# Gate logits of a mixture of experts as eight extra columns of the local attention's products

## The chip, the cores and the metric

The kernel runs on one core of a Trainium2 chip. The metric is device time in microseconds (us), as the median of several runs. One further execution was recorded by the hardware profiler; all durations of single instructions come from that one.

## The reference

A small early-fusion model, 16 sequences of 569 rows of 256 numbers, all f32. 441 rows come from image patches (a convolution and one attention head), 128 from text. Layer 0 is what matters here:

```python
h = concatenate([tokenizer(x), txt], axis=1)
h = h + local_attention(layernorm(h))        # windows of 64, shifted by 32, 8 heads
z = layernorm(h)                             # (h - mean) / sqrt(var + 1e-5), no weights
logits = z @ gate_w + gate_b                 # gate_w is 256 x 8
probs = softmax(logits)                      # 8 experts; the two largest are used
h = h + sum_e weight_e * (gelu(z @ W1_e + b1_e) @ W2_e + b2_e)
```

Layer 1 is a linear attention over phases followed by an LSTM over the 569 steps; neither is touched.

Because the layer norm subtracts the mean of a row, the logits can be written without the normalized rows: with `G` the gate weights less the mean of each column, `logits = rstd * (h @ G) + gate_b`. And h after the attention is `h0 + A @ w_out + biases`, so `h @ G = h0 @ G + A @ (w_out @ G) + biases @ G`. The windows already hold the normalized h0, turned, as an operand of TensorE: `h0 @ G = std0 * (layernorm(h0) @ G)`.

## The kernel before

The program has two parts. The first part (to about 950 us) makes the tokens, the window attention and the routing of the rows to experts. The second part runs the experts (79 tiles of 256 rows), then layer 1 and the LSTM.

**Order.** Every engine has a fixed order of instructions, which the program itself works out while it is built. `Order` is a planner: each piece of work is a generator ("stream") that yields an engine and an assumed duration before it issues instructions, for example `yield "PE", 0.44, "64"` (the last word names the tiling mode of TensorE's array, whose changes the planner charges for). The planner always takes next the step that can start first by its own clock. A changed step therefore also changes the order of others. `yield "at", event` waits for a mark that another stream sets; this is order only, the waits on the chip follow from the data.

**Units.** Two sequences make a pair `p` (8 pairs); a pair has 9 chunks of 128 rows, so there are 72 chunks. `H[p, c]` is a chunk's rows, 128 x 256, in 18 rotating buffers.

**Streams of the first part.**

- `setup` is not a stream: it is issued ahead, in program order. It loads the weights, multiplies constant weights together, and makes the bias rows `tok_b` and `win_b` (lines 484 to 490). The tiles of its pool give their room to those of the streams when setup's last use of them is over.
- `features` makes the image features `fT` for each sequence, on ScalarE (ACT, line 505) and VectorE (DVE, line 512); `projections` and two `tokens` streams turn them into rows of `H`.
- `norms` runs the first layer norm of each chunk (`norm`, lines 625 to 638): statistics on DVE, `rstd` on GpSimd (POOL, lines 635 and 636), the normalized rows `wxn` on DVE (line 638). It may be four chunks ahead of the windows.
- Four `windows` streams take the chunks in turn. Each turns `wxn` on TensorE (PE) into `xT`, makes keys and queries (`wqk`), scores (`wsc`), values (`wv`), a softmax over `wS` (DVE, POOL, ACT, DVE), turns it (`wpt`), multiplies by the values (`wav`), and by `wout` (`wob`, line 777); line 779 adds that to `h` in place. All of one stream's products share one PSUM bank, in turn. `h` is stored to `HD` in DRAM by a DMA of SyncE's queue (SP).
- A fork after each chunk, `sent_rows`, runs the second layer norm into `XN`.
- `routing` (lines 785 on) waits for a part's chunks and computes their logits: for two chunks at a time it turns `XN` on PE (`rtr`, line 800) and copies it on ACT (`rxT`, line 804); for up to four chunks it multiplies with the gate weights `gw` in the 32-column mode (`lg`, line 810), copies on ACT (`lgs`, line 816), turns back on PE (`lt`, line 819) and adds the bias on DVE (`pr`, line 821). Then come the softmax over 8 experts and the ranks on DVE, two products that count rows (`pos`), and the scatter of the rows to the experts' regions by POOL's indirect DMAs (`send`, line 908). A part is a pair; the last pair is cut into three parts of 4, 3 and 2 chunks, which makes 10 parts.

When the last part is routed, DVE works out which expert each tile belongs to, SP reads that into registers and fetches weights (line 1168) and rows (line 1174).

Of the kernel before, what the change touches and what calls it, by code (L numbers as in the profile page):

```python
# [17 lines left out]
D = 256  # L18
# [17 lines left out]
    ("bk1", 2), ("bq1", 2), ("bk2", 1), ("bq2", 1), ("ln_w", 2), ("ln_b", 2),  # L36
# [258 lines left out]
def kernel(ctx: ExitStack, tc: tile.TileContext, a: dict, out: bass.AP):  # L295
# [63 lines left out]
    gw = route.tile([128, 2, 32], F32, name="gw")  # L359
# [16 lines left out]
    H, XN, made = {}, {}, []  # L376
# [12 lines left out]
    def rows_of(p, c):  # L389

        while len(made) >= ROWS:
            before = ("normed", *made[len(made) - ROWS])
            if before in first.events:
                break
            yield "at", before
        made.append((p, c))
        H[p, c] = hp.tile([128, D], F32, name=f"h{p}_{c}", tag="h", bufs=ROWS)
        return H[p, c]

    def texts():  # L400

        for p in range(NP):
            if p:
                yield "at", ("token", p - 1, 3)
            for c in (7, 6, 8):
                h = yield from rows_of(p, c)
                if c == 8:
                    yield "POOL", 0.3
                    nc.gpsimd.memset(h, 0.0)
                lo, hi, at = {6: (25, 64, 0), 7: (0, 64, 39), 8: (0, 25, 103)}[c]  # L410
                for s in range(2):
                    nc.sync.dma_start(
                        h[64 * s + lo : 64 * s + hi], a["txt"][2 * p + s][at : at + hi - lo, :]
# [3 lines left out]
    def setup():  # L417
# [12 lines left out]
        nc.scalar.dma_start(wout, a["w_out"].rearrange("(k p) n -> p k n", p=128))  # L430
# [8 lines left out]
        nc.gpsimd.memset(gw, 0.0)  # L439
        nc.scalar.dma_start(gw[:, :, :E], a["gate_w"].rearrange("(k p) n -> p k n", p=128))  # L440
# [42 lines left out]
        for i, (name, w, b, to) in enumerate((("bv", wo, "bo", tok_b), ("vb", wout, "b_out", win_b))):  # L483
            v = tmp.tile([128, 2, 128], F32, name=f"{name}_every")
            for k in range(2):
                nc.vector.tensor_copy(v[:, k, :], col(name, k).to_broadcast([128, 128]))
            mm = place_of(f"{name}_row", 2 + i)
            for k in range(2):
                nc.tensor.matmul(mm[:, :D], v[:, k, :], w[:, k, :], start=(k == 0), stop=(k == 1))
            nc.vector.tensor_tensor(to, mm[:, :D], row(b), ALU.add)  # L490
# [77 lines left out]
    def tokens(slot):  # L568

        last = NIMG - 384  # L570
        for n in range(slot, 7 * NP, 2):
# [46 lines left out]
            for q, i in to:  # L618
                yield "DVE", 0.48
                nc.vector.scalar_tensor_tensor(  # L620
                    H[p, i][q], mm[q], share_[q], tok_b[q], ALU.mult, ALU.add
# [3 lines left out]
    def norm(h, to, name, slot):  # L625
# [3 lines left out]
        nc.vector.bn_stats(st, h)  # L629
# [4 lines left out]
        yield "POOL", 0.85  # L634
        nc.gpsimd.tensor_scalar(rstd, mv[:, 1:2], EPS, None, ALU.add)
        nc.gpsimd.tensor_tensor(rstd, rstd, mhalf[:, :1], ALU.pow)
        yield "DVE+", 0.5
        nc.vector.tensor_scalar(to, h, mv[:, 0:1], rstd, ALU.subtract, ALU.mult)
# [12 lines left out]
    def sent_rows(p, c, h, slot):  # L651

        if p not in XN:
            if p > 1:
                yield "at", ("sent", p - 2)
            if p not in XN:
                XN[p] = xnp.tile([128, NC, WIDE], F32, name=f"XN{p}", tag="XN", bufs=2)
                yield "POOL", 0.2
                nc.gpsimd.tensor_copy(XN[p][:, :, D], cols[:, COL["row"] + NC * p : COL["row"] + NC * (p + 1)])
        yield from norm(h, XN[p][:, c, :D], f"r{p}_{c}", slot)  # L660
# [11 lines left out]
    def windows(slot):  # L672

        kb, vb = KB[slot], VB[slot]
        for n in range(slot, NC * NP, WINDOWS):
# [28 lines left out]
            nc.gpsimd.tensor_tensor(h, h, win_b, ALU.add)  # L704
# [16 lines left out]
            v = place_of(f"wv{u}", slot)[:, :D].rearrange("p (w n) -> p w n", w=2)  # L721
            for w in range(2):
                for k in range(2):
                    yield "PE", 0.22, "64"
                    for odd in range(2):
# [4 lines left out]
                        )  # L730
            top = wk.tile([128, NH], F32, name=f"wtop{u}", tag=f"wtop{slot}", bufs=1)
            yield "DVE", 0.68
            nc.vector.tensor_reduce(top, S, AX.X, ALU.max)
            for odd in range(2):
# [39 lines left out]
            ob = place_of(f"wob{u}", slot)[:, :D]  # L774
            for m in range(2):
                yield "PE", D * COLUMN
                nc.tensor.matmul(ob, AT[:, m, :], wout[:, m, :], start=(m == 0), stop=(m == 1))
            yield "DVE", 0.42
            nc.vector.tensor_tensor(h, ob, h, ALU.add)
            nc.sync.dma_start(HD[p][:, c, :], h)  # L780
# [4 lines left out]
    def routing():  # L785

        for p, lo, hi in PARTS:
            u, n = f"{p}_{lo}", hi - lo
            pr = wk.tile([128, n, E], F32, name=f"pr{u}", tag="pr", bufs=1)
            for g0 in range(lo, hi, 4):  # L790
                m = min(4, hi - g0)
                xT = wk.tile([128, 2, 4, 128], F32, name=f"rxT{p}_{g0}", tag="rxT", bufs=1)
                for c0 in range(g0, g0 + m, 2):
                    two = min(2, hi - c0)
# [1281 lines left out]
```

## Time and profile before

| | |
|---|---|
| median of 3 runs | 3378.91 us (3378.6 to 3380.3) |
| profiled execution | 3360.87 us, its span 3359.0 us |
| granted TensorE clock in it | 0.978 |
| PE busy | 3055.1 us, 91% of the span, 57536 instructions |
| DVE busy | 2027.2 us, 60% |
| ACT busy | 1471.9 us, 44% |
| POOL busy | 786.6 us, 23% |
| moved by DMA | 366.81 MB, mean 109 GB/s |

The span runs from the first to the last instruction of the profiled execution. In a group of instructions the busy time is the union of their spans; spans of neighbours on PE overlap, since matmuls are pipelined. "Idle before" is the time in which the engine stood still just ahead of an instruction, and the name after the arrow is what ended it.

### The profile page before, as it was taken

The page shows a single profiled execution, that of the slowest core. Times are in us where ns is not written, and L with a number is a line of the kernel's source. Part 1 is how long each engine was busy: PE and PEld are TensorE (multiplying, and loading weights), DVE is VectorE, ACT ScalarE, POOL GpSimd, SP SyncE. Part 2 cuts the span into 40 slices and gives each one's busy share as a digit, 9 for nine tenths or more (in the row PEclk, how much of TensorE's full clock was granted, in tenths as well). Part 3 has the DMA queues.
Part 4 walks back from the last instruction along what each step waited for, and adds up shares of the span by engine and source line. Part 5 has one row for each costly group of instructions (what it writes and reads, how often), then busy time and mean ns, then how long its engine had stood idle before and what let it go on. Part 6 is the DMA issues. An engine that isn't in the chain of part 4 may idle for free.

```text
span 3359.0 us, 134328 instructions
## 1 busy us (share of the span) xinstructions
PE 3055.1 (91%) x57536; PEld 2231.5 (66%) x57536; DVE 2027.2 (60%) x6787; ACT 1471.9 (44%) x5030; POOL 786.6 (23%) x1524
## 2 busy tenths in 40 slices
PE   5999999999859999997899999999999999999884
PEld 3666666666548888886566676766666666666652
DVE  4677777766732222222566777777777777766555
ACT  3545545454412222221444555555555555554442
POOL 1243554445533322232311001010101010100000
PEclk9999999999979999998999999999999999999997
DMA  5111221111176666664333333333333333333333
GB/s 180 53 46 57 89 79 54 55 38 41 42 251 234 220 231 225 225 229 141 100 100 88 90 82 86 84 94 78 97 77 92 84 93 79 76 91 80 90 103 113
DMA packets 276070, 366.81 MB, mean 109 GB/s; under 512 B 144480, under 2 KB 220176, under 8 KB 263312
## 3 DMA queue, kind: packets, MB, share of 16 engines
q1 hardware_dynamic: 249360, 300.91, 30.5%
q0 software_dynamic: 14496, 39.75, 3.1%
q10 hardware_dynamic: 11616, 17.56, 1.8%
q8 instruction: 451, 7.39, 0.9%
q14 instruction: 147, 1.20, 0.1%
HBM read 239.33 MB, written 118.75 MB: 107 GB/s over the span
## 4 chain that ended last, share of the span: by engine, by line
PE 37%; DVE 7%; ACT 5%; issue 2%; SPq 1%; DMA 1%; POOL 0%; ACTq 0%; DVEq 0%; POOLq 0%
PE gates L1741 13%; PE xm_False L1085 5%; PE out_gate L1750 2%; PE ek L1085 2%; PE po_False L1085 2%; PE z L1085 2%; PE v L1085 2%; PE eq L1085 2%; PE ds_False L1085 2%; ACT act L1762 1%; PE r_False L1085 1%; ACT th L1798 1%; DVE ab L1777 1%; DVE cT L1790 1%; DVE act L1783 1%
## 5 line engine op out<-in xcount | busy, mean ns | idle before, releaser
L1741 PE MATMUL gates<-W_hh,X 128*16 128x96 f32 (+1 forms) x18176 | 487.9, 248 | 63.9 <-DVE X L1805 61.6
L1741 PEld LDWEIGHTS gates<-W_hh,X 128*16 128x16 f32 (+1 forms) x18176 | 373.6, 103 | 258.5 <-DVE X L1805 245.0
L1248 ACT ACTIVATE hT<-hp,w 128x256 f32<-128x256 f32 x316 | 132.6, 472 | 481.5 <-PE hp L1241 314.5
L1762 ACT ACTIVATE act<-gates 128x96 f32<-128x96 f32 x568 | 142.1, 250 | 444.1 <-PE gates L1741 437.0
L1255 PE MATMUL y<-w,hT 128*128 128x256 f32 x1264 | 289.7, 382 | 5.2 <-ACT hT L1248 1.5
L1085 PE MATMUL xm_False<-W_ih,dxT_False 128*32 128x256 f32 x4352 | 292.3, 380 | 2.3 <-DVE dxT_False L1271 1.9
L1241 PE MATMUL hp<-xt,w 128*128 128x256 f32 x1264 | 287.6, 381 | 1.0 <-ACT hT L1248 1.0
L1777 DVE SCALAR_TENSOR_TENSOR ab<-act 128x64 f32<-128x64 f32 x568 | 127.9, 225 | 258.2 <-ACT act L1762 250.8
L1255 PEld LDWEIGHTS y<-w,hT 128*128 128x128 f32 x1264 | 236.8, 190 | 45.2 <-ACT hT L1248 14.4
L1684 PEld LDWEIGHTS <-nil 128*32 128x32 bf16 x4552 | 190.3, 94 | 111.0 <-issue 53.0
L1241 PEld LDWEIGHTS hp<-xt,w 128*128 128x128 f32 x1264 | 239.9, 191 | 35.7 <-ACT hT L1248 1.5
L1184 POOL DMA_INDIRECT YT<-ys,to x158 | 153.4, 971 | 440.4 <-DVE ys L1261 408.9
L1261 DVE TENSOR_TENSOR ys<-y,w 128x512 f32<-128x512 f32 x79 | 54.6, 691 | 316.3 <-PE y L1255 241.1
L1750 PE MATMUL out_gate<-W_hh,X 128*32 128x64 f32 x9088 | 233.8, 219 | 0.7 <-issue 0.7
L1690 ACT COPY gates<-xc 128x96 f32<-128x96 f32 x569 | 138.6, 244 | 182.0 <-DMA xc<-XCD 75.4
L1750 PEld LDWEIGHTS out_gate<-W_hh,X 128*32 128x32 f32 x9088 | 187.9, 110 | 2.9 <-issue 1.1
L1805 DVE SCALAR_TENSOR_TENSOR X<-toT,th 128x32 f32<-128x32 f32 x569 | 109.9, 193 | 120.5 <-ACT th L1798 116.9
L1798 ACT ACTIVATE th<-cT 128x32 f32<-128x32 f32 x569 | 130.5, 229 | 92.9 <-DVE cT L1790 43.1
L1301 POOL TENSOR_SCALAR d_False_rstd<-d_False_mv 128x2 f32<-128x2 f32 (+1 forms) x36 | 9.0, 250 | 671.8 <-DVE d_False_mv L1293 547.4
L908 POOL DMA_INDIRECT XS<-XN,at x144 | 149.1, 1035 | 45.6 <-issue 24.6
L693 PE MATMUL wqk<-wxT,wqkv 128*128 128x128 f32 x1152 | 150.6, 278 | 8.9 <-ACT wxT L687 8.6
L693 PEld LDWEIGHTS wqk<-wxT,wqkv 128*128 128x128 f32 x1152 | 139.4, 192 | 24.9 <-ACT wxT L687 13.5
(356 smaller groups left out, 6497.9 us busy)
## 6 DMA issues: line engine op xcount, KB each, us to landing
w<-in_wpack SPq DMA_DIRECT2D x79, 1154.0 KB
taps<-in_taps SPq DMA_DIRECT2D x16, 1764.0 KB
xc<-XCD SPq DMA_DIRECT2D x71, 384.0 KB
XCD<-xp_False SPq DMA_DIRECT2D x256, 96.0 KB
xs<-XS SPq DMA_DIRECT2D x79, 258.0 KB
yg<-YT SPq DMA_DIRECT2D x72, 256.0 KB
HD<-h SPq DMA_DIRECT2D x72, 128.0 KB
fh<-HD SPq DMA_DIRECT2D x72, 128.0 KB
```

The costliest lines, as they stand in the source:

```text
L693: nc.tensor.matmul(qk[:, j, m, :], wqkv[:, k, D * j + 128 * m : D * j + 128 * m + 128], xT[:, k, :], start=(k == 0), stop=(k == 1),)
L908: fill(0, nc.gpsimd.indirect_dma_start(out=XS[0], out_offset=bass.IndirectOffsetOnAxis(ap=at[:, i, c - lo : c - lo + 1], axis=0), in_=XN[p ...
L1085: nc.tensor.matmul(out[own], lhsT[:, own], rhs, start=start, stop=stop)
L1184: keep(nc.gpsimd.indirect_dma_start(out=YT, out_offset=bass.IndirectOffsetOnAxis(ap=to[:, i : i + 1], axis=0), in_=ys[:, i, :], in_offset= ...
L1241: nc.tensor.matmul(hp[:, i, :], w1[:, k, hc * 128 : (hc + 1) * 128], xT[:, k, :], start=(k == 0), stop=(k == 1),)
L1255: nc.tensor.matmul(y[:, i, :], hT[:, hc, 128 * i : 128 * i + 128], w2[:, hc, :], start=(hc == 0), stop=(hc == 3),)
L1684: nc.tensor.matmul(g[32 * q : 32 * q + 32, :n], nil[:, :32], nil[:, :n], start=True, stop=last)
L1741: nc.tensor.matmul(GC[32 * q : 32 * q + NB * (1 + half), :96], before[:, kk, NB * (1 - half) :], Whh[:, kk, own : own + 96], start=False, ...
L1750: nc.tensor.matmul(GO[32 * q : 32 * q + 32, :64], before[:, kk, :], Whh[:, kk, own : own + 64], start=False, stop=(kk == 1),)
L1762: nc.scalar.activation(act[:, :96], GC[:, :96], AF.Tanh, scale=0.5), begun.pop((k, t))
L1777: nc.vector.scalar_tensor_tensor(ab, act[:, :64].rearrange("p (g x) -> p g x", g=2), 1.0, act[:, 64:].rearrange("p (g x) -> p g x", g=2), ...
L1798: nc.scalar.activation(th.rearrange("p k x -> p (k x)"), cT, AF.Tanh, scale=0.5)
```

## The change

The gate weights are centred once, in setup, by a product with a matrix of ones and two VectorE operations. `wout` gets eight more columns, `w_out @ G`, by two turns, two copies and two products for each of its halves; `win_b` gets eight more elements, the biases times `G`.

`H` gets nine more columns: eight for the growing logits and one for the standard deviation of the row before the attention. The first layer norm computes that one on POOL, by a third instruction after `rstd`. A window multiplies its `xT` with the centred gate weights just after the values, into eight more columns of the same PSUM bank, and VectorE scales them by the standard deviation and adds the bias. The product with `wout` and the add after it are 264 columns wide instead of 256. After the second layer norm a VectorE operation multiplies by `rstd` and adds `gate_b`, into a new tile `LG`. `routing` reads `LG` and has no step on PE or ACT ahead of its softmax.

```diff
-    gw = route.tile([128, 2, 32], F32, name="gw")
+    gw = route.tile([128, 2, E], F32, name="gw")
...
-        H[p, c] = hp.tile([128, D], F32, name=f"h{p}_{c}", tag="h", bufs=ROWS)
+        H[p, c] = hp.tile([128, D + E + 1], F32, name=f"h{p}_{c}", tag="h", bufs=ROWS)
...
# setup
-        nc.gpsimd.memset(gw, 0.0)
-        nc.scalar.dma_start(gw[:, :, :E], a["gate_w"].rearrange("(k p) n -> p k n", p=128))
+        nc.scalar.dma_start(gw, a["gate_w"].rearrange("(k p) n -> p k n", p=128))
...
+        nc.vector.memset(half, 0.5)
+        mm = place_of("gate_sum", 4)
+        for k in range(2):
+            nc.tensor.matmul(mm[:, :E], ones, gw[:, k, :], start=(k == 0), stop=(k == 1))
+        for k in range(2):
+            nc.vector.scalar_tensor_tensor(
+                gw[:, k, :], mm[:, :E], -1.0 / D, gw[:, k, :], ALU.mult, ALU.add
+            )
+        for m in range(2):
+            mm = place_of(f"wout_t{m}", 5)
+            woutT = tmp.tile([128, 2, 128], F32, name=f"woutT{m}")
+            for k in range(2):
+                nc.tensor.transpose(
+                    mm[:, 128 * k : 128 * k + 128], wout[:, m, 128 * k : 128 * k + 128], ident
+                )
+            nc.scalar.copy(woutT.rearrange("p k n -> p (k n)"), mm[:, :D])
+            mm = place_of(f"wout_gate{m}", 4)
+            for k in range(2):
+                nc.tensor.matmul(mm[:, :E], woutT[:, k, :], gw[:, k, :], start=(k == 0), stop=(k == 1))
+            nc.scalar.copy(wout[:, m, D:], mm[:, :E])
+        every = {}
+        for name in ("bv", "vb", "ob"):
...
+        mm = place_of("bv_row", 2)
+        for k in range(2):
+            nc.tensor.matmul(mm[:, :D], every["bv"][:, k, :], wo[:, k, :], start=(k == 0), stop=(k == 1))
+        nc.vector.tensor_tensor(tok_b, mm[:, :D], row("bo"), ALU.add)
+        mm = place_of("vb_row", 3)
+        for k in range(2):
+            nc.tensor.matmul(mm[:, : D + E], every["vb"][:, k, :], wout[:, k, :], start=(k == 0), stop=False)
+        for k in range(2):
+            nc.tensor.matmul(
+                mm[:, D : D + E], every["ob"][:, k, :], gw[:, k, :], start=False, stop=(k == 1)
+            )
+        nc.vector.tensor_tensor(win_b[:, :D], mm[:, :D], row("b_out"), ALU.add)
+        nc.vector.tensor_copy(win_b[:, D:], mm[:, D : D + E])
...
# norm
-        yield "POOL", 0.85
-        nc.gpsimd.tensor_scalar(rstd, mv[:, 1:2], EPS, None, ALU.add)
-        nc.gpsimd.tensor_tensor(rstd, rstd, mhalf[:, :1], ALU.pow)
+        yield "POOL", 0.85 if name[0] == "r" else 1.28
+        over = mv[:, 1:2]
+        nc.gpsimd.tensor_scalar(over, over, EPS, None, ALU.add)
+        nc.gpsimd.tensor_tensor(rstd, over, mhalf[:, :1], ALU.pow)
+        if name[0] == "w":
+            nc.gpsimd.tensor_tensor(h[:, D + E :], over, half, ALU.pow)
...
# sent_rows
-        yield from norm(h, XN[p][:, c, :D], f"r{p}_{c}", slot)
+        rstd = yield from norm(h, XN[p][:, c, :D], f"r{p}_{c}", slot)
+        yield "DVE", 0.19
+        nc.vector.scalar_tensor_tensor(
+            LG[p][:, c, :], h[:, D : D + E], rstd, frow("gate_b", E), ALU.mult, ALU.add
+        )
...
# windows, after the products of v
+            for k in range(2):
+                yield "PE", 0.06, "64"
+                for w in range(2):
+                    own = slice(64 * w, 64 * w + 64)
+                    nc.tensor.matmul(
+                        vg[own, D : D + E], xT[:, k, own], gw[:, k, :], start=(k == 0), stop=(k == 1)
+                    )
             top = wk.tile([128, NH], F32, name=f"wtop{u}", tag=f"wtop{slot}", bufs=1)
             yield "DVE", 0.68
             nc.vector.tensor_reduce(top, S, AX.X, ALU.max)
+            yield "DVE", 0.2
+            nc.vector.scalar_tensor_tensor(
+                h[:, D : D + E], vg[:, D : D + E], h[:, D + E :], win_b[:, D:], ALU.mult, ALU.add
+            )
...
-            ob = place_of(f"wob{u}", slot)[:, :D]
+            ob = place_of(f"wob{u}", slot)[:, : D + E]
             for m in range(2):
-                yield "PE", D * COLUMN
+                yield "PE", (D + E) * COLUMN
                 nc.tensor.matmul(ob, AT[:, m, :], wout[:, m, :], start=(m == 0), stop=(m == 1))
             yield "DVE", 0.42
-            nc.vector.tensor_tensor(h, ob, h, ALU.add)
-            nc.sync.dma_start(HD[p][:, c, :], h)
+            nc.vector.tensor_tensor(h[:, : D + E], ob, h[:, : D + E], ALU.add)
+            nc.sync.dma_start(HD[p][:, c, :], h[:, :D])
...
# routing
-            pr = wk.tile([128, n, E], F32, name=f"pr{u}", tag="pr", bufs=1)
-            for g0 in range(lo, hi, 4):
-                m = min(4, hi - g0)
-                xT = wk.tile([128, 2, 4, 128], F32, name=f"rxT{p}_{g0}", tag="rxT", bufs=1)
-                for c0 in range(g0, g0 + m, 2):
...
-                            nc.tensor.transpose(
-                                tr[:, k, c - c0, :], XN[p][:, c, 128 * k : 128 * k + 128], ident
-                            )
...
-                    nc.scalar.copy(xT[:, :, c0 - g0 : c0 - g0 + two, :], tr[:, :, :two, :])
...
-                        nc.tensor.matmul(
-                            lg[32 * j : 32 * j + 32, :128], gw[:, k, :], xT[:, k, j, :],
-                            start=(k == 0), stop=(k == 1),
-                        )
...
-                nc.scalar.copy(lgs[: 32 * m], lg[: 32 * m, :128])
...
-                nc.tensor.transpose(lt, lgs[: 32 * m], ident[: 32 * m, : 32 * m])
...
-                nc.vector.tensor_tensor(
-                    pr[:, g0 - lo : g0 - lo + m, :],
-                    lt.rearrange("p (j e) -> p j e", e=32)[:, :, :E],
-                    frow("gate_b", E).unsqueeze(1).to_broadcast([128, m, E]), ALU.add,
-                )
+            for c in range(lo, hi):
+                yield "at", ("normed", p, c)
+            pr = LG[p][:, lo:hi, :]
```

## The prediction

> **What bounds the kernel now.** I read first the 40 slices of the span, to find where the change lives. A digit is the busy share in tenths; a slice is 84 us.
>
> ```profile
> PE   5999999999859999997899999999999999999884
> DVE  4677777766732222222566777777777777766555
> POOL 1243554445533322232311001010101010100000
> ```
>
> The changed work lies in slices 0 to 11, the first stage: tokens, windows, routing. There TensorE (PE) is at nine tenths, VectorE (DVE) at seven and GpSimd (POOL) at four or five. Second, the busy time of the stage's steady part as one stretch:
>
> ```profile
> core 0: us, PE busy (x) PEld busy (x) DVE busy (x) ACT busy (x) POOL busy (x), PEclk, DMA share, GB/s
> 60.00:900.00 840.00, 781.04 (x6887) 547.65 (x6888) 595.54 (x1556) 421.40 (x1144) 376.23 (x658) 1.00 0.17 58
> ```
>
> PE is busy 781 of 840 us and DMA 17%, so PE bounds this stretch, with 59 us of gaps. DVE follows at 71%, ACT at 50%, POOL at 45%. Third, PE's waits there (us in total, times, longest):
>
> ```profile
> PE wpt L754 <- DVE wS L750: 10.0, 9, 2.5
> PE wv L726 <- DVE wS L717: 9.4, 10, 1.9
> PE wqk L693 <- ACT wxT L687: 7.4, 13, 1.4
> PE wtr L683 <- DVE wxn L638: 6.2, 8, 1.6
> ```
>
> The gaps are the windows' own chains, mostly DVE's part of them. The routing's turned rows and gate products are not among the large waits: what they cost is PE time. Fourth, the groups by shape (60 to 950 us): busy time, mean ns of one, idle time before.
>
> ```profile
> L800 PE MATMUL rtr<-ident,XN 128*128 128x128 f32 x144 | 26.3, 287 | 1.3 <-DVE part L887 0.6 <-DVE XN L638 0.5
> L810 PE MATMUL lg<-rxT,gw 128*32 128x128 f32 x288 | 15.7, 283 | 0.9 <-ACT rxT L804 0.7
> L819 PE MATMUL lt<-ident,lgs 128*128 128x128 f32 x15 | 4.8, 323 | 1.5 <-ACT lgs L816 1.5
> L766 PE MATMUL wav<-wPT,VB 128*64 128x64 f32 x1152 | 48.2, 227 | 3.4 <-ACT wPT L759 3.4
> L777 PE MATMUL wob<-wout,wAT 128*128 128x256 f32 x288 | 75.2, 387 | 1.1 <-ACT wAT L773 0.9
> L636 POOL TENSOR_TENSOR w_rstd<-w_rstd,mhalf 128x1 f32<-128x1 f32 x71 | 44.2, 622 | 5.9
> ```
>
> The counts show that one f32 product is two instructions (288 for 144 products) and a turn is one. Neighbours overlap, so group sums are too large; I take the step from start to start in the order of time where I can. Last, the two ends of the stage in order of time (start, us), setup first:
>
> ```profile
> 28.66 0.26 DVE L462 TENSOR_TENSOR mixed<-mixed,ew 128x96 f32<-128x96 f32 x1
> 29.11 2.08 PE L489 MATMUL bv_row<-tok_wo,bv_every 128*128 128x256 f32 x4 [4.55 <-DVE bv_every L486]
> 31.88 2.04 PE L489 MATMUL vb_row<-wout,vb_every 128*128 128x256 f32 x4 [0.70 <-issue]
> 33.97 1.96 ACT L505 ACTIVATE fT<-taps,cols 128x220 f32<-128x220 f32 x4 [9.00 <-PE vb_row L489]
> ```
> ```profile
> 936.36 0.57 POOL L636 TENSOR_TENSOR r_rstd<-r_rstd,mhalf 128x1 f32<-128x1 f32 x1
> 940.11 1.08 PE L800 MATMUL rtr<-ident,XN 128*128 128x128 f32 x4 [0.56 <-DVE part L887]
> 943.41 0.36 PE L819 MATMUL lt<-ident,lgs 64*128 64x64 f32 x1 [0.41 <-ACT lgs L816]
> 963.40 0.91 SPq L1168 DMA_DIRECT2D w<-in_wpack  x2
> ```
>
> At the front the first features wait for setup's last product (9.00 us of ACT's time), so setup is serial. At the back, the last part's logits pass turn, copy, product, copy, turn before DVE can rank them, and the experts' weights are fetched 20 us after that. Setup and tail are latency; the middle is PE throughput.
>
> **What the Trainium skill says.** TensorE: Matmul & The Clock Gate, "LDWEIGHTS (loading the stationary operand)": the load takes about its columns over 1.2 ns, 53 ns for 64 columns. The trace pays less when two 64-column tiles alternate: 64 of wav took 2.01 us from start to start, 31 ns each. TensorEngine Tiling (Array Packing), "Key Properties": a change of tiling mode drains the engine. That agrees in direction: the 32-column gate group costs 0.58 us for 16 instructions (412.65 to the next start at 413.23) and 0.55 us for four (423.37 to 423.92), so most of it is not the products. SBUF — State Buffer, "SBUF: two separate sides": VectorE and GpSimd share a port pair that one of them holds for a whole instruction. The trace shows no such wait by name, so I use it only as a reason for a bound.
>
> **The change part by part.** PE, removed: 144 turns; four took 0.49 us (407.66 to 408.15), so 0.12 x 144 = 17.6 us. 24 gate groups x 0.57 = 13.6. 24 turns back x 0.16 (413.76 to 413.91 and alike) = 3.8. Sum 35 us; the group sums (26.3 + 15.7 + 7.2 = 49) are the upper bound.
>
> PE, added: per chunk two k by two windows, twice for f32, so 8 instructions of 128x64 weights and 8 moving columns, 576 in all. No row has this shape; wav is nearest (same weights, alternating halves, 64 columns) at 31 to 39 ns (2.01/64, 0.63/16). Fewer columns can't beat the load, so I take 35: 20.2 us. Ends: 26 ns, the out_gate products (233.8 us over 9088, 32 columns), 14.8 us; 53 ns, the page's price without overlap, 30.7 us. They follow v's products in the same mode, so I add no switch. The out product grows from 256 to 264 columns: 14 of wob took 3.12 us, 0.87 ns a column, x 8 x 288 = 2.0 us. Net on PE: 35 - 22.2 = **13 us less** (2 to 32).
>
> ACT loses 40 copies of rxT and 24 of lgs, about 28 us; I count nothing, since it is half idle; a shorter ACT queue can only help the 23 us of PE's waits on it. DVE gains two small products per chunk: 144 x 0.19 (the 128x8 reciprocal's 194 ns) = 27 us, less 24 adds (4 us): +23 us, 71 to 74%. POOL gains a third power per chunk in the windows' norms, 72 x 0.57 = +41 us, 45 to 50%. Both lie beside PE's work. Their cover is the four window and two token streams; without it they lengthen the DVE waits above. The new power is queued behind rstd, so DVE's wxn need not wait for it, but POOL's next instruction does (h plus win_b, the softmax subtraction). The new DVE product waits for the gate products; behind it in DVE's order stand the other windows' copies and sums. Against that, DVE no longer stands still for the turned-back logits (7.8 us before 900). I take 0, with -6 to +15.
>
> DMA: the gate weights' load stays at its place on ACT's queue, but setup needs it now instead of at 149 us. Its landing is not shown; the core's traffic is near nothing after 27 us, so it should be there before 28.9. SP's stores of h carry the same 256 columns. The memset of gw on POOL goes, 0.15 us, at a time when POOL is early.
>
> Setup: after "mixed" DVE centres the gates (two, about 0.4 us); then PE product, ACT copy, PE turn, ACT copy, PE product, ACT copy: about 0.5 + 0.3 + 0.5 + 0.5 + 0.6 + 0.3 = 2.7 us on rows of the same setup (four qb products 0.50 us, copies 0.17 to 0.38). The bv row thus starts near 31.9 instead of 29.1, both rows follow back to back (4.2 us instead of 4.8), and four short products with gw close it (0.5 us). The end moves from 33.9 to some 36.7: **+3 us**, ends 0 (PE's clock already up) and +6 (late gate weights). Nothing covers it.
>
> Tail: from the last part's XN (937.4) to its logits (943.8) stand 6.4 us. Now one DVE product of 0.19 us remains, but DVE still has the previous part to finish (941.3), so some 2.5 us come off there. The part before waited 2.7 us for its turned-back logits, and its scatter on POOL held back the last chunk's rstd (DVE waited 2.7 us for it). What is late next is that scatter, 1.27 us a piece. I take **-4 us**, ends -7 and +2.
>
> Sum: -13 + 0 + 3 - 4 = **-14 us**. The profiled execution took 3360.87 us (span 3359.0 plus 1.9), so 3346.9 there. The median of the runs, 3378.91, is 18 us above it, which no part of the change touches; carried over, 3364.9. A measurement of this kernel can tell about 0.2%, 6.8 us, from no change.
>
> **The rivals.** (1) The sum holds, -7 to -22: 50%. (2) The drains are worth the group sums and the routing leaves the streams' way: 49 - 17 on PE, 3 and -4 at the ends, about -30, 3349: 14%. For it: the 32-column group's flat 0.55 us. (3) Cover: PE's removed pieces filled gaps of the window chains, whose length does not change. Then some 5 of the 13 us arrive, -6 in all, 3373, within what can be told: 20%. For it: 59 us of gaps, nearly all in those chains. Against: PE is at 93%. (4) Slower: DVE and POOL take over. Place: wxn and the softmax subtraction behind the third power, on queues where DVE already waits 19.2 us for w_rstd. Price: 41 + 23 = 64 us of new work; from 21 us of it showing up as PE gaps (a third) the kernel is slower by over 0.2%, at half (32) by 18 us, 3397: 16%. Against: the norms run up to four chunks ahead. That the change doesn't do what it says is no case: the routing's PE steps are gone from the code.
>
> **How the numbers follow.** The likeliest is 3365. The range 3350 to 3385 leaves out about half of (2) and most of (4). Faster 0.64 is (1) and (2), same 0.20 is (3), slower 0.16 is (4).
>
> **What would show it.** Right: rtr, lg, lt gone; 576 small products at 30 to 40 ns from start to start; the first fT near 37 us; PE busy some 13 to 25 us less before the experts; weights fetched about 14 us earlier than 963.4. Wrong: small products above 53 ns, more PE waits on wS and wxn, POOL as their releaser, or a later stage moving by more than the first one's shift.

## The result, and the profile after

The change makes the kernel faster by 0.44%: 3363.13 us (median of 6 runs, 3361.35 to 3367.92) against 3378.76 us for the kernel before beside it (6 runs, 3374.59 to 3382.14), ratio 0.9956, 95% interval 0.9943 to 0.9968. That is 15.6 us less, where the forecast was 14 less and 3365. The profiled execution took 3363.40 us, its span 3361.6.

One caution before the lines are read. Another session of runs can give the same kernel some 12 us more or less: before had medians of 3368.94, 3380.29 and 3367.60 in the three sessions of experiments (the first two on one chip, the third on another), while the ratio of the two kernels was 0.9956 here and 0.9958 and 0.9954 in the two sessions in which the change was run again. So total times are compared below only within one session, and the start times in the profile of before quoted in the prediction (3360.87 us) are not set against those of this one of after: their experts start at 972.8 and 971.9 us, which hides nearly the whole gain. A pair from one session follows the views of after.

The page of after, the 40 slices (a digit is the busy share in tenths, a slice is 84 us):

```profile
PE   6999998999759999997899999999999999999884
DVE  4777777786732222222566777777777777776555
POOL 1354465545533322222311001010101010100000
```

POOL rises by one tenth in six of the slices 1 to 8 and falls by one in slice 4, DVE hardly changes, PE not visibly. The shape is that of before. After's steady part as one stretch:

```profile
core 0: us, PE busy (x) PEld busy (x) DVE busy (x) ACT busy (x) POOL busy (x), PEclk, DMA share, GB/s
60.00:900.00 840.00, 777.30 (x7058) 547.92 (x7056) 619.97 (x1676) 397.50 (x1085) 427.25 (x751) 0.99 0.17 60
```

PE is still the bound at 93%. DVE is up 24 us and POOL 51, ACT down 24 against the same stretch of before. After's waits of PE in this stretch (us in total, times, longest):

```profile
PE wav L816 <- ACT wPT L809: 10.6, 16, 1.4
PE wqk L731 <- ACT wxT L725: 7.2, 12, 1.2
PE wpt L804 <- DVE wS L800: 6.3, 10, 1.2
PE wv L765 <- DVE wS L755: 6.0, 14, 0.8
```

The waits on DVE's `wS` became smaller (10.0 and 9.4 us before). At the head stands a wait on ACT's copy of the turned softmax, 2.8 us before. No releaser is POOL. After's groups by shape (60 to 950 us; busy, mean ns of one, idle time before and what ended it):

```profile
L787 ACT COPY VB<-wv 64x256 f32<-64x256 f32 x144 | 52.2, 366 | 135.3 <-DVE h L781 119.3 <-DVE ahead L882 7.2 <-DVE wtop L779 4.1
L668 POOL TENSOR_TENSOR h<-w_mv,half 128x1 f32<-128x1 f32 x71 | 41.8, 589 | 0.0
L774 PE MATMUL wv<-gw,wxT 128*64 128x8 f32 x576 | 26.1, 196 | 0.0
L696 DVE SCALAR_TENSOR_TENSOR LG<-h,r_rstd,flow 128x8 f32<-128x8 f32 x72 | 18.4, 256 | 0.3
L781 DVE SCALAR_TENSOR_TENSOR h<-wv,h,win_b 128x8 f32<-128x8 f32 x72 | 15.5, 218 | 14.4 <-PE wv L774 5.5 <-PE tav L636 3.4 <-remote 1.9
```

`rtr`, `lg` and `lt` are gone, and the 576 small products are there with no idle time ahead of them. Their 26.1 us are spans that overlap those of their neighbours. Their price is seen in after's order of time (start, duration in us):

```profile
416.17 1.09 PE L765 MATMUL wv<-wqkv,wxT 128*64 128x128 f32 x16
417.09 0.35 PE L774 MATMUL wv<-gw,wxT 128*64 128x8 f32 x8
417.38 2.67 PE L636 MATMUL tav<-tV,tPT 57*64 57x256 f32 x20
...
435.22 1.09 PE L765 MATMUL wv<-wqkv,wxT 128*64 128x128 f32 x16 [0.51 <-DVE wS L755]
436.14 0.35 PE L774 MATMUL wv<-gw,wxT 128*64 128x8 f32 x8
436.35 1.06 PE L749 MATMUL wsc<-KB,wq 128*64 128x256 f32 x8
```

From start to start, eight products take 0.21 us when the next work has weights of the same 128x64 shape (436.14 to 436.35) and 0.29 us when the shape changes (417.09 to 417.38). Over the chunks where PE did not stand still behind them the median is 0.20 to 0.21, three quarters are at 0.28 or less. That is 26 ns a product and 15 to 17 us in all.

After's setup in order of time:

```profile
34.48 0.86 PE L515 MATMUL vb_row<-gw,ob_every 128*128 128x8 f32 x4
...
35.43 1.96 ACT L534 ACTIVATE fT<-taps,cols 128x220 f32<-128x220 f32 x4 [4.21 <-PE vb_row L515]
```

The end of the chain is as foreseen: the short products close it, and the first features stand behind them, at 35.4 us.

Now the pair of one session: before run again as `b_third` (median 3367.40) and the change as `a_third` (3354.57). Three stretches: first features to the last attention product of the token part (`tav`); to the last store of `h`; to the experts' first turn of rows. First before, then the change, columns as above (PEclk is the granted TensorE clock, 1.00 the full one):

```profile
33.90:873.80 839.90, 780.36 (x6751) 543.78 (x6753) 587.63 (x1533) 422.95 (x1148) 362.20 (x632) 0.99 0.18 61
873.80:935.00 61.20, 42.65 (x430) 32.16 (x426) 47.20 (x138) 23.65 (x59) 41.81 (x75) 0.94 0.17 60
935.00:974.00 39.00, 4.58 (x22) 3.37 (x22) 15.34 (x77) 4.07 (x13) 16.28 (x30) 0.51 0.82 278
```
```profile
34.90:866.20 831.30, 769.88 (x6960) 540.38 (x6960) 620.42 (x1676) 401.69 (x1096) 411.34 (x724) 1.00 0.18 63
866.20:925.70 59.50, 41.19 (x360) 31.25 (x356) 41.91 (x135) 19.55 (x50) 38.19 (x67) 0.85 0.15 54
925.70:956.50 30.80, 1.03 (x4) 0.95 (x5) 11.95 (x56) 3.23 (x11) 8.56 (x16) 0.50 0.85 270
```

The lengths give the account: setup +1.0, the middle 839.9 to 831.3, -8.6, the last windows -1.7, the tail 39.0 to 30.8, **-8.2**. The experts start 17.5 us earlier.

The split between the first two stretches can't be used as it stands, because the clock differs. The trace records TensorE's clock as granted in full or at half. In the middle, before had half of it in two stretches (33.9 to 48.6 and 461.6 to 468.4 us), the change in one; PE's busy time in them, first before, then the change:

```profile
sum 21.50, PE 14.06 PEld 7.97 DVE 17.20 ACT 8.41 POOL 7.18; mean PE 7.03 PEld 3.98 DVE 8.60 ACT 4.21 POOL 3.59
37.50:44.30 6.80, 3.73 (x6) 1.63 (x6) 5.61 (x16) 2.54 (x6) 2.18 (x4) 0.50 0.46 145
```

PE's work at full clock can be estimated by counting its busy time at half clock as half. The middle then has 773.3 us of PE work before and 768.0 in the change: 5.3 us less, where the busy times say 10.5. The estimate can be tested: the three profiles of before have 778.0, 780.2 and 780.4 us of PE in their middles, and 773.4 to 773.6 at full clock. In the last windows the clock tips the other way, 0.94 before and 0.85 in the change: half clock for 6.8 us in each of the three profiles of before, for 17.8 to 26.8 us in those of the change. Taken together the two stretches had half clock for nearly the same time, 28.3 us before and 24.6 in the change, and can be compared: they are 10.3 us shorter, **901.1 to 890.8**. At full clock PE's work there falls by 11.8 us, 813.8 to 802.0, and its gaps grow by 1.6, 78.1 to 79.7.

How much the gaps grow is the less certain part. The other two profiles of the change have the same PE work at full clock (802.0 and 802.2 us), but gaps of 84.9 and 82.9 us. They come from sessions in which the change took 9 to 13 us more and before 3379 and 3380 us; no profile of before has a total near that.

The stages behind are the same program. In this pair they took 9.3 us longer after the change (2396.3 against 2387.0), with PE at half clock for 95.7 us of them against 69.4. So the span is only 8.2 us shorter in these two profiles, while the medians differ by 13.0.

In the tail, the change (same run) in order of time:

```profile
925.74 0.32 SPq L830 DMA_DIRECT2D HD<-h  x1
...
927.35 0.41 DVE L670 TENSOR_SCALAR XN<-h,r_mv,r_rstd 128x256 f32<-128x256 f32 x1 [1.00 <-POOL r_rstd L666]
...
927.68 0.22 DVE L696 SCALAR_TENSOR_TENSOR LG<-h,r_rstd,flow 128x8 f32<-128x8 f32 x1
...
933.39 0.17 DVE L1117 CAST behind<-place 128x8 int32<-128x8 f32 x1
```

and before:

```profile
934.98 0.32 SPq L780 DMA_DIRECT2D HD<-h  x1
...
939.62 0.41 DVE L638 TENSOR_SCALAR XN<-h,r_mv,r_rstd 128x256 f32<-128x256 f32 x1 [2.71 <-POOL r_rstd L636]
...
942.77 1.09 PE L800 MATMUL rtr<-ident,XN 128*128 128x128 f32 x4 [0.56 <-DVE part L887]
...
946.07 0.36 PE L819 MATMUL lt<-ident,lgs 64*128 64x64 f32 x1 [0.41 <-ACT lgs L816]
...
951.94 0.17 DVE L1100 CAST behind<-place 128x8 int32<-128x8 f32 x1
```

From the last store of `h` to `XN` it is 1.6 us instead of 4.6; from `XN` to the logits 0.3 us instead of 6.9 (the bias add stands at 946.48); from there to the ranks' last step 5.7 against 5.5. Together 9.3 us less on a serial path; from there to the experts' first turn it takes 1.0 us longer, which leaves the 8.2.

### The profile page after: what moved, and what is told of

Its sections match the earlier page's. It is cut to its first block, busy times and chain, and to the rows that moved or that the text cites. A ratio compares the mean times of both kernels' runs of the same rounds, so it can differ in the third digit from the quotient of the medians.

```text
span 3361.6 us, 134719 instructions
## 1 busy us (share of the span) xinstructions
PE 3057.9 (91%) x57676; PEld 2233.4 (66%) x57676; DVE 2051.8 (61%) x6913; ACT 1445.8 (43%) x4970; POOL 825.3 (25%) x1595
## 4 chain that ended last, share of the span: by engine, by line
PE 37%; DVE 7%; ACT 4%; issue 2%; SPq 1%; DMA 1%; POOL 0%; ACTq 0%; DVEq 0%; POOLq 0%
PE gates L1758 13%; PE xm_False L1102 5%; PE out_gate L1767 2%; PE po_False L1102 2%; PE z L1102 2%; PE ek L1102 2%; PE v L1102 2%; PE ds_False L1102 2%; PE eq L1102 1%; ACT act L1779 1%; PE r_False L1102 1%; ACT th L1815 1%; DVE ab L1794 1%; DVE cT L1807 1%; DVE act L1800 1%
```

## The experiments

The theory was the prediction's: PE work taken away is what shortens the middle, setup costs a little, the tail gains a little. The rivals were the drains of the 32-column mode (bigger gain), pieces that only filled gaps (smaller), and POOL and DVE as new bounds. One thing makes this kernel awkward to experiment on: a planner writes the order of the instructions from planned durations (the `yield` lines), so an edit can change the order of everything behind it.

**Before, once more** (session 1), no edit.

> The kernel before, unchanged, with another profile. Two theories of why the two profiles show the first stage ending 0.3 us apart (first expert weights asked for at 963.4 and at 963.1 us) while the medians lie 15.6 us apart. Theory A: the profiled execution of the kernel before was a lucky one, 18 us under its own median; then a second profile has a span near 3377 us and the first expert weights at about 975 to 980 us. Theory B: profiling itself changes the time of the kernel before; then the second profile again shows about 3359 us while the timed runs stay near 3379.

3367.72 against 3368.94 us, ratio 0.9997 (0.9989 to 1.0005). The profile has a span of 3367.2 us and starts the experts at 974.3 us, 1.5 us after the first profile of before: that one was the shorter mostly behind this point (2386.2 against 2392.8 us), not in the first stage.

**The change's setup alone, in the kernel before** (session 1).

```diff
-        for i, (name, w, b, to) in enumerate((("bv", wo, "bo", tok_b), ("vb", wout, "b_out", win_b))):
+        mm = place_of("gate_sum", 4)
...
-                nc.tensor.matmul(ob, AT[:, m, :], wout[:, m, :], start=(m == 0), stop=(m == 1))
+                nc.tensor.matmul(ob, AT[:, m, :], wout[:, m, :D], start=(m == 0), stop=(m == 1))
```

> The kernel before with only the setup of the change: centred gates, wout with eight more columns that nothing reads, the longer bias row; the routing multiplies with the centred gates, which gives the same logits since normalized rows have no mean. The forecast's setup term: +3 us (0 to +6). From the trace of the change, where the first features start at 35.4 instead of 34.0 us: +1.5 us. If order and chance matter more than the sum, it lies anywhere within 10 us.

3373.97 us, ratio 1.0012 (1.0005 to 1.0020): +4 us by the ratio, with the first features at 36.2 us against 32.7 in the run of before in that session, +3.5. Only setup differs between the two in the order of instructions. The experts start at 977.5 us against 974.3, so what setup costs is still there at the end of the stage.

**Before without its routing products** (session 1): the logits come from the rows' first eight columns, so turns, gate products, turns back and their copies are left out.

```diff
-            for g0 in range(lo, hi, 4):
...
+            for c in range(lo, hi):
+                yield "at", ("normed", p, c)
+            pr = LG[p][:, lo:hi, :]
```

> The kernel before with the routing's turned rows, gate products and copies taken out and nothing in their place but the VectorE product after the second norm, which reads the first eight numbers of h (so the logits are not those of the reference). It shows the removal alone. The forecast: 35 us off PE and 4 off the tail, so -39 us if PE's time converts in full; -22 to -30 if the windows' chains keep part of it. The rival that PE's removed pieces filled gaps: -15 or less.

3347.87 us, ratio 0.9939 (0.9925 to 0.9952): 20.6 us less by the ratio. That is what the removal may bring with nothing added, but the planner wrote a new order, so it is not a clean price; `b_held` below is.

**The change, with DVE's read of the logits behind ACT's copies** (session 1). In the profile of the change ACT waits long for that read; both read the same PSUM bank.

```diff
-            nc.vector.scalar_tensor_tensor(h[:, D : D + E], vg[:, D : D + E], ...)
             for odd in range(2):
                 nc.scalar.copy(vb[own, :, :, odd, :], ...)
+            nc.vector.scalar_tensor_tensor(h[:, D : D + E], vg[:, D : D + E], ...)
```

> The change with one step moved: VectorE reads the gate products after ACT's two copies of v out of the same PSUM bank, not before them. In the trace of the change ACT stands still 119 us ahead of these copies until that VectorE read is over (49 us before, until PE). If this wait is on the path: 5 to 15 us faster than the change, near 3350. If ACT's idle time is off the path (it is half idle): the same as the change within 5 us, 3363.

3369.12 us, ratio 1.0001 (0.9992 to 1.0009): no gain on the change but all of its advantage lost. ACT's largest waits ahead of these copies, before (`b_third`), the change (`a_third`) and this kernel, each to the start of its last `tav`:

```profile
ACT VB L737 <- PE wv L726: 42.9, 33, 3.0
```
```profile
ACT VB L787 <- DVE h L781: 108.4, 44, 5.1
```
```profile
ACT VB L783 <- PE wv L774: 80.8, 47, 3.8
```

The wait on DVE went, and 80.8 us of waiting for PE stood in its place. So in this order the copies were not late because of DVE alone. Since the order changed everywhere too, the 15 us cannot be laid on this edit's own work.

**The change once more** (session 2), no edit.

> The change itself, unchanged, once more beside the kernel before on one chip. The two profiles put the start of the experts only 1 us apart (first turn of expert rows at 972.8 and 971.9 us), the medians 15.6 us. Theory A: the gain lies in the first stage and the profile of before was a lucky execution: then -14 to -16 us again, and a second profile starts the experts 10 to 15 us ahead of the kernel before. Theory B: the first stage gains little, and most of the 15.6 us was made in the later stages, which run the same program and whose length depends on chip and execution: then the ratio comes out between -6 us and 0 here, and the experts start within 4 us of 974.3, where the second profile of the kernel before has them.

3367.32 against 3380.29 us, ratio 0.9958 (0.9945 to 0.9971). The gain came again, as theory A has it; the experts start at 968.6 us, 5.7 us ahead of `b_again`, less than theory A asked. The two profiles are of different sessions, which is why a pair of one session was taken later.

**The change without the third power** (session 2): the standard deviation is left out and a constant scales the logits.

```diff
-        yield "POOL", 0.85 if name[0] == "r" else 1.28
+        yield "POOL", 0.85
...
-        if name[0] == "w":
-            nc.gpsimd.tensor_tensor(h[:, D + E :], over, half, ALU.pow)
```

> The change without the third power on POOL in the windows' norms (the gate products are scaled by 0.5 instead of the row's standard deviation, so the logits are not the reference's). POOL has 42 us less. Forecast's step (hidden behind rstd): the same as the change within 4 us. The rival that POOL's queue is what gives the gain back: 10 to 20 us faster than the change.

3381.43 us, ratio 1.0005 (0.9997 to 1.0013): 14 us *more* than the change, with 42 us of POOL's work gone. No theory of a resource gives that.

**The change with its gate products twice** (session 2).

```diff
+            for again in range(2):
             for k in range(2):
                 yield "PE", 0.06, "64"
                 for w in range(2):
                     nc.tensor.matmul(vg[own, D : D + E], xT[:, k, own], gw[:, k, :], ...)
```

> The change with each chunk's gate products issued twice into the same columns: 576 more small products, 26 ns each in the trace, so 15 us more of PE time and nothing else. If PE's time converts in full, +15 us against the change; if half of it falls into gaps, as the removal alone suggests (35 us off PE gave 21 us), +8; if the gaps take it all, 0.

3393.05 us, ratio 1.0035 (1.0022 to 1.0048): 25.7 us more than the change, for some 16 us of PE. Both of these kernels have another order of instructions from the first fifth of the stage on.

**Order alone** (session 2): in the kernel before, one planned duration changed, and no instruction.

```diff
-            yield "POOL+", 0.8
+            yield "POOL+", 0.74
             nc.gpsimd.tensor_tensor(h, h, win_b, ALU.add)
```

> The kernel before with one planned duration changed (0.74 instead of 0.8 us for POOL's addition of the bias to h; the profile has 0.73), no instruction added or taken away. It shows what a mere change of the planner's order is worth in the first stage. If the sum of the parts is to be trusted to a few us, within 4 us of the kernel before; if order weighs as much as the parts, 5 to 15 us either way.

3384.19 us, ratio 1.0012 (1.0005 to 1.0018): 4 us for nothing but another order. So `a_no_power`, `a_gates_twice`, `a_read_late` and `b_no_gates` show part and order together. The first of them suggests that an order can outweigh 42 us of work on POOL. Session 3 therefore kept the order: the `yield` lines stay and only the instructions go.

**The pair of session 3**, no edits.

> The kernel before, unchanged, a third profile, beside the change on the same chip. Its medians so far were 3369 and 3380 us in two sessions, and its two profiles (3360.87 and 3368.94) start the experts at 972.8 and 974.3 us. If the first stage is what varies between sessions: where the timed runs lie near 3380, the experts start near 985. If it is the later stages: the experts start at 973 to 975 whatever the total, and the time from there to the end varies by 10 us.

> The change, unchanged, a third time, for a pair of profiles of one session. If the gain belongs to the change: -13 to -16 us against the kernel before whatever that takes here. If it depends on the session: about 3365 us where the kernel before takes 3369, so -4 us, and 3366 where it takes 3380.

3367.40 us, ratio 1.0004 (0.9996 to 1.0012); and 3354.57 us, ratio 0.9954 (0.9941 to 0.9967). The gain keeps its size where before takes 3367 us, so it belongs to the change and not to the session.

**Before without the routing's products and copies, order held** (session 3). The turns, gate products, turns back, copies and the load of the gate weights are left out; the bias is added to the rows' first columns. Every other instruction stands in before's order on PE, ACT, DVE and POOL.

```diff
                             yield "PE", TURN
-                            nc.tensor.transpose(tr[:, k, c - c0, :], XN[p][...], ident)
...
                     yield "PE", 0.24, "32"
-                    nc.tensor.matmul(lg[32 * j : 32 * j + 32, :128], gw[:, k, :], xT[:, k, j, :], ...)
...
                 yield "DVE", 0.2
-                nc.vector.tensor_tensor(pr[...], lt.rearrange(...)[:, :, :E], ...)
+                nc.vector.tensor_tensor(pr[...], XN[p][:, g0 : g0 + m, :E], ...)
```

> The kernel before without the routing's turned rows, gate products, turned-back logits and their copies, while the planner is still told of them with the same durations, so that all other instructions keep their order on every engine; VectorE's add of the gate bias reads the first eight normalized numbers (the logits are not the reference's). It shows the removed PE work alone, without another order. The forecast's 35 us on PE and 4 to 6 us of the tail: -39. If the windows' chains keep half: -20. If the removal's -21 us in the freely planned version came from a lucky order: -10 or less.

3356.19 us, ratio 0.9964 (0.9951 to 0.9977): 11.4 us less than before. Its middle, columns as above, then PE's busy time at half clock over the middle and the last windows, first before (`b_third`), then this kernel:

```profile
34.10:859.90 825.80, 756.45 (x6353) 522.72 (x6354) 588.45 (x1533) 402.25 (x1092) 364.69 (x632) 0.98 0.18 62
```
```profile
sum 28.30, PE 18.43 PEld 11.20 DVE 21.59 ACT 9.37 POOL 12.88; mean PE 6.14 PEld 3.73 DVE 7.20 ACT 3.12 POOL 4.29
sum 50.50, PE 36.48 PEld 24.16 DVE 35.75 ACT 16.67 POOL 30.95; mean PE 5.21 PEld 3.45 DVE 5.11 ACT 2.38 POOL 4.42
```

The middle is 14.1 us shorter than before's, but the last windows are 3.2 us longer (64.4 against 61.2), and this kernel ran at half clock for 50.5 us of the two, before for 28.3. All five of its runs had a mean clock of 0.971 to 0.974, where before's median was 0.976; whether the edit brings that about is not shown. At full clock PE has 30.4 us less to do in the two stretches, its gaps grow by 10.5 us (78.1 to 88.5), and they would be 19.9 us shorter. So about a third of the time taken off PE became waiting for the windows' chains.

Its tail in order of time:

```profile
927.03 0.41 DVE L635 TENSOR_SCALAR XN<-h,r_mv,r_rstd 128x256 f32<-128x256 f32 x1 [0.77 <-POOL r_rstd L633]
...
931.15 0.16 DVE L880 CAST at<-slot 128x6 int32<-128x6 f32 x1
931.22 0.17 DVE L801 TENSOR_TENSOR pr<-XN,flow 128x16 f32<-128x16 f32 x1
```

From the last `h` to the ranks it takes 12.4 us (924.3 to 936.7) against 17.0, which is 4.6 us less, where the change has 9.3 less. No part waits for turned-back logits here, and still DVE finishes the previous part (its last step is at 931.15) before it takes up the last part's logits, since it stands there in before's order: 4.2 us from `XN` to the logits, against 6.9 before. In the change that last step of the previous part is at 921.17, 4.6 us ahead of the last store of `h`. So half of what the tail gains on this path is the removal's (to the experts' first turn it is 3.0 us of 8.2); the other half goes with the place that the planner gave the previous part.

**The change without its gate products, order held** (session 3). The products are left out and DVE reads eight columns of the values; the rest is in the change's order.

```diff
                 yield "PE", 0.06, "64"
-                for w in range(2):
-                    nc.tensor.matmul(vg[own, D : D + E], xT[:, k, own], gw[:, k, :], ...)
...
-                h[:, D : D + E], vg[:, D : D + E], h[:, D + E :], win_b[:, D:], ALU.mult, ALU.add
+                h[:, D : D + E], vg[:, :E], h[:, D + E :], win_b[:, D:], ALU.mult, ALU.add
```

> The change without its 576 small products, while the planner is still told of them, so that every other instruction keeps its place; VectorE reads eight columns of v in their stead (the logits are not the reference's). It shows what these products cost in the change: 16 us of PE at the trace's 0.22 us a chunk. In full: -16 us against the change, near 3350; half: -8; none: 0. The version that issues them twice was 26 us slower than the change, with another order; if order made 10 us of that, half or full is to be expected here, not more.

3345.30 us, ratio 0.9940 (0.9927 to 0.9953): 9.3 us less than the change by the medians, 5 by the ratios. Its middle:

```profile
34.90:858.50 823.60, 758.34 (x6416) 523.72 (x6416) 622.25 (x1676) 401.07 (x1095) 410.39 (x723) 0.99 0.18 64
```

The middle is 7.7 us shorter than in `a_third`, middle and last windows together 8.0 (882.8 against 890.8). At full clock, estimated as above, PE has 14.2 us less to do in the two stretches, its gaps are 4.1 us longer, and the small products cost the stage 10.0 us.

The windows then add up, in time at full clock over the two stretches: -19.9 for what was removed, +10.0 for the gate products, and -0.2 left over to come to the change's -10.1. PE's work: -30.4 and +14.2, and +4.4 left over to come to -11.8. In that rest lie the wider output product (+2.0 estimated) and the new order; they were not parted from each other. The rest in time is small, but with the order worth several us either way that may be a balance of larger parts.

The medians alone do not add up like this: -11.4 and +9.3 leave -2.1, where the change has -13.0. The clocks of the runs differ. Brought to one mean clock by the 1.4 us per 0.001 of the last section (an estimate), the means of the runs put `b_held` 17.0 us below before, `a_held` 9.2 below the change and the change 13.8 below before. With 5.2 us for the other half of the tail and +1.0 to +3.5 for setup, the parts come to -10 to -12.

## Why the prediction was right, point by point

**The sum held, but through two errors of opposite sign.** Forecast were -13 for the middle, 0 for DVE and POOL, +3 for setup and -4 for the tail. In the pair of session 3 the windows (middle and last) gave -10.3, setup +1.0 and the tail -8.2. That the windows fell short by about as much as the tail exceeded its term is luck. The signs that the prediction named came near: the first features at 34.9 to 36.2 us (37), PE busy 15.5 us less from the first features to the experts (13 to 25), the weights fetched at 947.78 instead of 964.66 us in the pair, 16.9 earlier (14). The small products missed theirs, 26 ns instead of 30 to 40.

**"Sum 35 us" removed from PE: a little too large.** Held in order, the removal takes 30.4 us off PE's work at full clock in the windows and 1.3 in the tail, 31.7 in all. The terms came from pieces picked out of the order of time, start to next start. Perhaps part of such a step is filling and draining that the next piece pays anyway; no run parts the two.

**"Fewer columns can't beat the load, so I take 35": too dear.** Measured 26 ns, the forecast's lower end; leaving the products out takes 14.2 us off PE's work, where 20.2 was counted. The 53 ns of a load is not what a product costs here. The nearer statement stands elsewhere on the same page: the Trainium skill, TensorE: Matmul & The Clock Gate, "Back-to-back issue gap", gives 1 to 64 moving columns one price, an issue floor of about 25 ns, for products without their loads. The trace agrees for eight columns, with the loads: 0.20 to 0.21 us for eight products. `wav`, taken as the nearest row, has 64 moving columns and lies above that floor, at 31 ns.

**"Net on PE 13 us less" as a gain in time.** PE's work at full clock did fall by 11.8 us in the windows, close to 13, because both terms were too large by a similar amount (35 against 31.7 removed, 22.2 against 18.6 added). In this pair 10.1 of them reached the length. Part by part it was less: 30.4 us taken away gave 19.9, and 14.2 put in cost 10.0, about two thirds, though PE is busy 93% of the middle. This is **rival 3** as a part of the truth: the removed pieces did fill gaps, some 10 us worth, which the forecast set at nothing within its main case. Its reading that the 59 us of gaps lie nearly all in the windows' chains was loose, too: in the list of PE's waits before, about 43 of 58 us do, the rest belongs to the token streams and the routing.

**DVE and POOL at 0: no cost shown.** The power measures 41.8 us in its group against 41 forecast, and its idle time is 0.0: it runs when its turn comes and waits for nobody. DVE's small operations take 218 and 256 ns instead of 194, 34 us instead of 27. The prediction's own tests speak against **rival 4**: PE's waits on `wS` fell, none is released by POOL, and DVE's wait of `wxn` for `w_rstd` went down from 19.2 to 5.6 us. `a_no_power` can't be read either way.

**A wait that was not foreseen.** "The new DVE product waits for the gate products" was right and small (5.5 us); what waits for *it* was missed. ACT's copies of the values read the same bank and stand behind DVE's read for 108 to 119 us, where before they waited 43 to 49 us, nearly all for PE. The Trainium skill, PSUM — Partial Sum Buffer, "PSUM bank collisions raise a hardware error", says that no two engines may touch one bank in the same quadrant at once, reads included; so the two readers have to go one after the other. The traces agree: here ACT waits for DVE's read, and where DVE comes second (`a_read_late`) it waits for ACT's copies, 5.1 us. How much of ACT's wait is that turn, and how much is DVE's own lateness, was not measured. What followed is small: PE waits 10.6 us for ACT's `wPT`, before 2.8. That the first causes the second was not tried.

**Setup +3: right.** The first features came 3.5 us later with the new setup alone, which costs 4 us in all; half clock began at the same time in both of these profiles (29.6 and 29.7 us). In the pair of session 3 they came 1.0 us later, but before's setup there ran at half clock for 5.8 us and the change's for 3.4.

**Tail -4: half of what came.** In before's order (`b_held`) the removal is worth 4.6 us on the serial path, the forecast's size: 1.9 ahead of `XN`, and 2.7 between `XN` and the logits, where 2.5 was counted. The change has 9.3: the last chunk's `rstd` no longer stands behind the previous part's scatter, which is worth 3.0 us, and 6.5 of the 6.9 us between `XN` and the logits came off. The step "DVE still has the previous part to finish" held as long as the order did. In the planner's new order that part is done before the last store of `h`, which the forecast could have asked and did not.

**Rival 2** (the drains are worth more) is out: the order-held removal is below the 35 us (31.7), not above.

## What to carry to other kernels

Where a planner writes the order, the price of a part is found by leaving out its instructions and keeping its places; otherwise order alone (4 us here for one number, and more in others) passes for the part's cost. On an engine that is busy 93%, work taken off came back as time at about two thirds, and the serial end of the stage, with a few of its instructions, gave nearly as much as all its windows (8.2 against 10.3 us): walk such ends instruction by instruction, with the piece before the last one too. Before busy times of two profiles are subtracted, compare how long each ran at half clock: here that made half of the difference in the middle. Two kernels whose medians come from different sessions should be compared by their ratio to a common neighbour.

## What was not expected of the hardware

- 128x64 products with eight f32 columns issue every 25 to 26 ns when they alternate between column halves, and a change of the weights' shape behind them adds 0.08 us (0.20 against 0.28 us for the group of eight).
- The granted clock is not the same from run to run of one program, nor alike in its stages. In the middle stretch the three profiles of the change had half clock for 25.3, 13.7 and 6.8 us. In the last windows every profile of before had 6.8 us, every profile of the change 17.8 to 26.8, `b_held` 24.7 and `b_order`, before in another order, 17.1; what sets it was not tried. Among the runs of one kernel in one session, a mean clock lower by 0.001 went with about 1.4 us more (an estimate by a straight line through 227 runs).
- One program's time moved by about 11 us (3368.9 to 3380.3 us, 0.34%) between two sessions on the same chip. The median clock was 0.976 and 0.975, which by the line above makes 1 to 2 us of it. What causes the rest stays open.
